# Quarter-row gathers and 32x32 block transposes on VectorE for 44 of 64 experts

## The chip, the core and the metric

The kernel runs on one core of a Trainium2 chip. The core has a matrix engine (TensorE, PE in the profile; its weight loads are listed as PEld), a vector engine (VectorE, DVE), an activation engine (ScalarE, ACT), a general engine (GpSimd, POOL) and a sequencer that here only issues transfers (SyncE, SP). They run side by side, each through its own instructions in order, and wait for one another through semaphores. Sixteen DMA engines move data; SP, ACT and POOL put transfers on queues for them. Data lie in device memory (DRAM), in SBUF (128 partitions), or in PSUM, where TensorE writes its results. The metric is the time of one execution on the device in microseconds (us).

## The reference

One block of a transformer with adaptive normalisation, in float32, for 2048 tokens of 512 features:

```
h = layernorm(x) * (1 + ca) + sa
x = x + ga * attention(h)            # 16 heads of 128, causal
h = layernorm(x) * (1 + cb) + sb
x = x + gb * ffn(h)
```

and `ffn` is a mixture of 64 experts with two shared ones:

```
topk_scores, topk_idx = top_k(softmax(flat @ Wr + router_bias), 4)   # 4 of 64 experts per token
xb[e, pos] = flat[tok]                     # at most 128 tokens per expert
h  = silu(xb @ Wg) * (xb @ Wu)             # 512 -> 128, per expert
yb = h @ Wd                                # 128 -> 512
out[tok] += yb[eid, pos] * weight
hs = silu(flat @ Sg) * (flat @ Su)         # two shared experts of width 512
out += hs @ Sd
```

## The kernel before, in words

The first two thirds of the time are attention: projections, scores, softmax and weighted values, head by head. Its probabilities are transposed by VectorE in 32x32 blocks (`turn_blocks`, L466) after DMAs have swapped the blocks (L456); this is the one place where the kernel before uses that instruction.

**Router stage.** For each tile of 128 tokens, PE sums the attention's output over the heads (L936), VectorE adds it up and normalises it to `h` (`norm`, L747 to L763), and POOL's queue writes `h` to a DRAM tensor `h2d` (L762). `h` has four buffers. `turn_h` transposes `h` on PE into `h2T`, `logit` gives the router's logits, `choose`, `positions` and `seat_tokens` give every token a seat with its experts. After the last tile, `table` is copied to `tb`, and `tok` (L888) holds, for seat p of expert e, the number of the token. SP loads the attention's output for later tiles in this stage (`load_ab`, L572, tile `v`), the shared weights (L932, L933) and then the first three experts' weights.

**Experts.** An expert's rows are gathered by `load_xb` (L1211): an indirect DMA on POOL's queue reads 128 rows of 2 KB of `h2d` at the indices `tok[:, e]`, into one of three buffers `xb`, with a token on each partition. TensorE needs the features on the partitions, so `expert_turn` transposes four 128x128 pieces on PE into the PSUM tile `tpx` (L1221), and ACT copies them to `xbT` (L1223). `expert_up` (L1228) multiplies with the expert's two up weights `wgu` into the PSUM tile `pse`, which has one buffer; `glu` forms `he` from it (L987 on ACT, L988 and L989 on VectorE). `expert_mid` transposes `he` (L1243, `tph`), `expert_down` multiplies with `wd` (L1249, `psy`), VectorE scales it to `y` (L1251), and ACT's queue writes it to DRAM. The steps overlap: step e gathers for e + 3, transposes for e + 1, does the up projection of e, the middle of e - 1 and the down projection of e - 2.

**Order.** The order of these blocks is set in the program, not by priorities. Each step is a list of pairs (columns of PE work, function), and `merge` interleaves the list of the experts with that of the shared experts' work (`first` to `fourth`, tile `pst`, and `shared_down`, tile `psd`) so that both are done by the same share at any time. The cost 512 of a transpose counts in this. `tpx` and `tph`, like `table` before them, have the PSUM tag `tr` with two buffers.

**Combination.** When the experts are done, indirect DMAs gather the results by token (L1281), VectorE adds them up, and SP stores the output, beside the last shared work on PE.

Of the kernel before, what the change touches and what calls it, by code (L numbers as in the profile page):

```python
# [18 lines left out]
P = 128  # L19
# [4 lines left out]
def adaln_block_kernel(  # L24
# [41 lines left out]
    dram = ctx.enter_context(tc.tile_pool(name="dram", bufs=1, space=DRAM))  # L66

    ident = const.tile([P, P], F32)
# [9 lines left out]
    gb = const.tile([P, D], F32)  # L78
    atd = dram.tile([H, DH, N], F32)
    h2d = dram.tile([N, D], F32)  # L80
    ybd = dram.tile([E * CAP, D], F32)

    def merge(streams, marks):
# [40 lines left out]
    with ExitStack() as att:  # L124
# [63 lines left out]
        with tc.tile_pool(name="pre", bufs=1) as pre, tc.manual_schedule():  # L188
# [388 lines left out]
        xts = {}  # L577
# [113 lines left out]
    keep = ctx.enter_context(tc.tile_pool(name="keep", bufs=1))  # L691
# [8 lines left out]
    psO = ctx.enter_context(tc.tile_pool(name="psO", bufs=2, space=PSUM))  # L700
# [5 lines left out]
    rt = rts.enter_context(tc.tile_pool(name="rt", bufs=1))  # L706
# [4 lines left out]
    iota = rt.tile([P, E], F32)  # L711
    places = rt.tile([P, CAP], F32)
    own = rt.tile([P, 1], F32)
    tok = keep.tile([CAP, E], U32)
    hs_ = {}
    mvs = {}
    logits = {}
# [5 lines left out]
    def route_consts():  # L723
        nc.sync.dma_start(out=wr, in_=Wr.rearrange("(k p) e -> p k e", p=P))
        nc.sync.dma_start(out=rb, in_=router_bias.partition_broadcast(P))
        make_upper_triangular(nc, before, val=1.0, diag=False)
        nc.gpsimd.memset(onesb, 1.0)
        nc.gpsimd.iota(
            iota, pattern=[[1, E]], base=0, channel_multiplier=0,
            allow_small_or_imprecise_dtypes=True,  # L730
        )
        nc.gpsimd.iota(
            places, pattern=[[1, CAP]], base=0, channel_multiplier=0,
            allow_small_or_imprecise_dtypes=True,
        )
        nc.gpsimd.iota(
            own, pattern=[[0, 1]], base=0, channel_multiplier=1,
            allow_small_or_imprecise_dtypes=True,
        )

    def load_x(j):
        nc.sync.dma_start(
# [4 lines left out]
    def norm(t):  # L747

        st = rt.tile([P, 6], F32, name="st", bufs=3)
        nc.vector.bn_stats(st, acc[:, t, :])  # L750
        mv = rt.tile([P, 2], F32, name="mv", bufs=3)
        nc.vector.bn_aggr(mv, st)
        rstd = rt.tile([P, 1], F32, name="rstd", bufs=3)
        nc.scalar.activation(rstd, mv[:, 1:2], AF.Sqrt, bias=eps, scale=1.0)
        nc.vector.reciprocal(rstd, rstd)
        h = rt.tile([P, D], F32, name="h", bufs=4)
        nc.vector.tensor_scalar(
            h, acc[:, t, :], mv[:, 0:1], rstd, ALU.subtract, ALU.mult
        )
        nc.vector.tensor_mul(h, h, cb)  # L760
        nc.vector.tensor_add(h, h, sb)
        nc.gpsimd.dma_start(out=h2d[t * P : (t + 1) * P, :], in_=h)  # L762
        hs_[t] = h  # L763

    def turn_h(t):
# [105 lines left out]
    def seat_tokens(b):  # L871


        t0, nt = BLOCKS[b]
        seat, who = seats.pop(b)
        for n in range(nt * K):
            i, k = divmod(n, K)
            nc.tensor.matmul(
                out=table,
                lhsT=seat[:, n, :],  # L880
                rhs=who[:, i, k].rearrange("p j e -> p (j e)"),
                start=(b == 0 and n == 0),
                stop=(b == len(BLOCKS) - 1 and n == nt * K - 1),
            )
        if b == len(BLOCKS) - 1:
            tb = rt.tile([CAP, 2 * E], F32, name="tb")
            nc.vector.tensor_copy(tb, table)
            nc.vector.scalar_tensor_tensor(  # L888
                tok, tb[:, E:], float(P), tb[:, :E], ALU.mult, ALU.add
            )  # L890

    table = psO.tile([CAP, 2 * E], F32, name="table", tag="tr")
    ALL = ((0, 4), (4, 8), (8, 12), (12, 16))
# [12 lines left out]
    with tc.manual_schedule():  # L906
# [55 lines left out]
    with ExitStack() as ex:  # L962
# [241 lines left out]
        xbs = {}  # L1204
        xts = {}
        ups = {}
        hts = {}

        def load_xb(e):
            xbs[e] = xbp.tile([CAP, D], F32, name="xb", bufs=3)  # L1210
            nc.gpsimd.indirect_dma_start(  # L1211
                out=xbs[e][:, :],
                out_offset=None,
                in_=h2d[:, :],
                in_offset=bass.IndirectOffsetOnAxis(ap=tok[:, e : e + 1], axis=0),
            )

        def expert_turn(e):
            tp = psO.tile([P, DC, P], F32, name="tpx", tag="tr")
            for k in range(DC):  # L1220
                nc.tensor.transpose(tp[:, k, :], xbs[e][:, k * P : (k + 1) * P], ident)  # L1221
            xts[e] = xbp.tile([P, DC, CAP], F32, name="xbT")
            nc.scalar.copy(xts[e], tp)  # L1223

        def expert_up(e):
            ps = psO.tile([P, 2 * HE], F32, name="pse", tag="pl", bufs=1)
            for k in range(DC):
                nc.tensor.matmul(  # L1228
                    out=ps,
                    lhsT=xts[e][:, k, :],  # L1230
                    rhs=weights[e][:, k].rearrange("p i h -> p (i h)"),
                    start=(k == 0),
                    stop=(k == DC - 1),
                )
# [19 lines left out]
        def expert_step(e):  # L1254
            out = []

            def turn():
                if e + 3 < E:
                    load_xb(e + 3)
                expert_turn(e + 1)  # L1260

            def down():
                expert_down(e - 2)
                if e + 1 < E:
                    load_down(e + 1)

            if e + 1 < E:
                out.append((512, turn))
            if e < E:
                out.append((1024, lambda: expert_up(e)))  # L1270
            if 0 <= e - 1 < E:
                out.append((128, lambda: expert_mid(e - 1)))
            if e >= 2:
                out.append((512, down))
            return out
# [20 lines left out]
                store(t)  # L1296

        with tc.manual_schedule():
            for e in range(3):
                load_xb(e)  # L1300
            expert_turn(0)
            for j in range(1, 5):
                weight_sum(0, j)
            experts = []
            for e in range(E + 2):
                experts += expert_step(e)
            merge([experts, shared[LEAD:-TAIL]], [])
# [58 lines left out]
```

## Time and profile before

| | |
|---|---|
| median of 9 runs | 2494.81 us (2490.94 to 2496.55) |
| the profiled execution | 2488.51 us, span of its instructions 2486.7 us |
| granted TensorE clock, mean | 0.995 |
| PE busy | 2421.2 us, 97% of the span |
| DVE busy | 1518.7 us, 61% |
| ACT busy | 656.2 us, 26% |
| POOL busy | 224.4 us, 9% |
| gathers of rows, L1211 | 64, 1988.9 to 2329.1 us |
| transposes of gathered rows, L1221 | 256, 1993.4 to 2346.5 us |

An instruction's line in the profile names its engine, its line in the program (L1221), its operation, the tile it writes and those it reads (`tpx<-ident,xb`), and the shape. In lists of groups, the count follows, then the busy time, the mean duration in ns, and after a bar how long the engine stood idle just before these instructions and what ended that. In timelines a line begins with the start and the duration in us, and several instructions of one kind are put together (x4). A float32 matmul has two records, a transpose one. Durations of matmuls overlap, since they are pipelined. A row of the table by windows has the bounds of the window, its length, the busy time of each engine (with the number of instructions), the granted clock, the DMA engines' mean busy share and the GB/s they moved. A row of a DMA queue has packets, MB, and the share of 16 engines' time: q1 carries what SP issues, q0 what POOL issues, q10 what ACT issues. SPq, ACTq and the like are transfers being issued.

### The profile page before, as it was taken

What the parts mean: (1) busy time and instruction counts of PE and PEld (TensorE: products, weight loads), DVE (VectorE), ACT (ScalarE), POOL (GpSimd) and SP (SyncE); (2) the same over time, 40 slices, a digit from 0 to 9 for tenths busy, and PEclk for the clock granted to TensorE, in tenths of its full rate; (3) what the DMA queues carried; (4) which work ended last, traced back from release to release, by engine and by line L of the source; (5) the groups of instructions that cost most, each with busy time, mean ns of one, the idle gap of its engine ahead of it and who ended that gap; (6) DMA issues with size and microseconds to landing.
All of it is one profiled execution on the core that took longest, in us unless ns stands there. A gap on an engine that the chain in (4) does not pass through costs nothing.

```text
span 2486.7 us, 26246 instructions
## 1 busy us (share of the span) xinstructions
PE 2421.2 (97%) x8525; PEld 1524.7 (61%) x8525; DVE 1518.7 (61%) x2982; ACT 656.2 (26%) x1476; POOL 224.4 (9%) x286
## 2 busy tenths in 40 slices
PE   7999999999999999999999999899999999999999
PEld 4666666666666666666666666555544476877844
DVE  4466666676666666666666666676665562654654
ACT  3233333323322333333233333322111221222200
POOL 0000000000000000000000000000100021111073
PEclk9999999999999999999999999999999999999999
DMA  4234434444444444444444344565523277877664
GB/s 140 62 87 108 115 92 111 116 111 103 115 110 97 110 115 98 109 99 119 104 96 121 96 117 110 139 192 139 178 68 131 85 211 219 241 222 237 187 191 147
DMA packets 225952, 326.26 MB, mean 131 GB/s; under 512 B 32116, under 2 KB 140696, under 8 KB 225816
## 3 DMA queue, kind: packets, MB, share of 16 engines
q1 hardware_dynamic: 198936, 253.26, 39.3%
q0 software_dynamic: 17664, 54.54, 7.3%
q10 hardware_dynamic: 9216, 16.78, 1.8%
q8 instruction: 69, 1.13, 0.2%
q14 instruction: 67, 0.55, 0.1%
HBM read 139.91 MB, written 41.94 MB: 73 GB/s over the span
## 4 chain that ended last, share of the span: by engine, by line
PE 70%; DVE 16%; SPq 6%; issue 3%; DMA 3%; ACT 1%; POOL 1%; DVEq 0%; ACTq 0%; POOLq 0%
PE pqk L169 12%; PE ps L413 12%; PE po L484 11%; PE pso L936 6%; DVE pt L466 6%; PE pv L329 6%; SPq L456 6%; PE pse L1228 4%; PE pst L1083 4%; DVE nm L426 3%; PE psd L1145 3%; PE psg L999 3%; DVE p L402 2%; PE psy L1249 2%; PE psb L591 2%
## 5 line engine op out<-in xcount | busy, mean ns | idle before, releaser
L432 ACT ACTIVATE p<-ps,nm 128x1024 f32<-128x1024 f32 (+7 forms) x384 | 332.0, 864 | 1039.8 <-DVE nm L430 370.7
L484 PE MATMUL po<-pt,v 128*128 128x256 f32 (+1 forms) x2304 | 567.4, 368 | 7.3 <-DVE pt L466 3.6
L413 PE MATMUL ps<-kt,qt 128*128 128x512 f32 (+3 forms) x1280 | 532.7, 532 | 32.2 <-ACT p L432 31.3
L484 PEld LDWEIGHTS po<-pt,v 128*128 128x128 f32 x2304 | 425.6, 190 | 222.1 <-issue 156.0
L426 DVE TENSOR_REDUCE nm<-ps 128x1 f32<-128x1024 f32 (+7 forms) x384 | 349.5, 910 | 94.8 <-PE ps L413 86.0
L466 DVE STREAM_TRANSPOSE pt<-pt 128x1664 f32<-128x1664 f32 (+2 forms) x160 | 317.9, 1988 | 59.3 <-DMA pt<-p 54.2
L413 PEld LDWEIGHTS ps<-kt,qt 128*128 128x128 f32 x1280 | 234.8, 190 | 181.8 <-issue 127.3
L425 DVE TENSOR_TENSOR ps<-ps,causal 128x128 f32<-128x128 f32 x256 | 74.4, 291 | 348.8 <-PE ps L413 348.7
L329 PE MATMUL pv<-wv,hT 128*128 128x256 f32 x1024 | 240.3, 379 | 0.0
L169 PE MATMUL pqk<-hT,wk 128*128 128x512 f32 x512 | 233.2, 599 | 0.0
L169 PE MATMUL pqk<-hT,wq 128*128 128x512 f32 x512 | 231.7, 596 | 0.0
L494 POOL DMA_DIRECT2D atd<-at x128 | 79.1, 619 | 1676.5 <-ACT at L493 1653.6
L402 DVE TENSOR_SCALAR p<-p,rs 128x1024 f32<-128x1024 f32 (+7 forms) x384 | 218.0, 596 | 9.1
L329 PEld LDWEIGHTS pv<-wv,hT 128*128 128x128 f32 x1024 | 194.5, 190 | 31.0 <-issue 1.9
L936 PE MATMUL pso<-hT,v 128*128 128x512 f32 x384 | 173.7, 597 | 0.0
L169 PEld LDWEIGHTS pqk<-hT,wk 128*128 128x128 f32 x512 | 98.5, 193 | 103.6 <-issue 101.0
L169 PEld LDWEIGHTS pqk<-hT,wq 128*128 128x128 f32 x512 | 97.8, 191 | 98.4 <-issue 95.4
L1228 PE MATMUL pse<-wgu,xbT 128*128 128x256 f32 x512 | 121.1, 379 | 0.0
L936 PEld LDWEIGHTS pso<-hT,v 128*128 128x128 f32 x384 | 69.6, 190 | 71.5 <-issue 70.8
L1145 PE MATMUL psd<-wsd,hs 128*128 128x512 f32 x256 | 111.5, 592 | 0.0
L1228 PEld LDWEIGHTS pse<-wgu,xbT 128*128 128x128 f32 x512 | 93.8, 190 | 11.7 <-issue 1.0
L1211 POOL DMA_INDIRECT xb<-h2d,tok x64 | 65.0, 1015 | 302.1 <-PE tpx L1221 273.1
(258 smaller groups left out, 1930.2 us busy)
## 6 DMA issues: line engine op xcount, KB each, us to landing
pt<-p SPq DMA_DIRECT2D x768, 104.0 KB
pt<-p SPq DMA_DIRECT2D x256, 124.0 KB
pt<-p SPq DMA_DIRECT2D x256, 108.0 KB
atd<-at POOLq DMA_DIRECT2D x128, 128.0 KB
wgu<-in_L_ffn_Wg_dram SPq DMA_DIRECT2D x64, 256.0 KB
wgu<-in_L_ffn_Wu_dram SPq DMA_DIRECT2D x64, 256.0 KB
wd<-in_L_ffn_Wd_dram SPq DMA_DIRECT2D x64, 256.0 KB
ybd<-y ACTq DMA_DIRECT2D x64, 256.0 KB
```

Of the source, the lines that this page charges most:

```text
L169: nc.tensor.matmul(out=ps, lhsT=w[:, k, :], rhs=hTs[j][:, k, :], start=(k == 0), stop=(k == DC - 1),)
L329: nc.tensor.matmul(out=ps, lhsT=hTs[t // 4][:, k, (t % 4) * P : (t % 4 + 1) * P], rhs=wv[:, k].rearrange("p i d -> p (i d)"), start=(k == ...
L402: nc.vector.tensor_scalar(cols[:, :, a:b], cols[:, :, a:b], rs[:, n : n + 1], None, ALU.mult)
L413: nc.tensor.matmul(out=ps[:, o : o + wo], lhsT=q, rhs=kts[hd, (c0 + o) // 512][:, :wo], start=True, stop=True,)
L426: nc.vector.tensor_reduce(nm[:, n : n + 1], ps[:, :w], AX.X, ALU.max, negate=True)
L432: nc.scalar.activation(rows[:, r0 + c0 // P : r0 + (c0 + w) // P], ps[:, :w].rearrange("q (r b k) -> q r b k", b=4, k=32), AF.Exp, bias=nm ...
L456: nc.sync.dma_start(out=pt[32 * b : 32 * (b + 1), a * w : (a + 1) * w], in_=pb[32 * a : 32 * (a + 1), b * w : (b + 1) * w],)
L466: nc.vector.transpose(part, part)
L484: nc.tensor.matmul(out=po if wide else po[:, P:], lhsT=vts[g][:, kt, hh * DH : (hh + 1) * DH], rhs=rows[:, r : r + last + 1 : last] if wid ...
L936: nc.tensor.matmul(out=ps, lhsT=abs_[pr][:, hd, i * P : (i + 1) * P], rhs=wos[hd // 4][:, hd % 4, :], start=(hd == 0), stop=(hd == H - 1),)
L1145: nc.tensor.matmul(out=ps, lhsT=hsh[b, f][:, i * P : (i + 1) * P], rhs=wsd[:, f, :], start=(f == 0), stop=(f == NHC - 1),)
L1228: nc.tensor.matmul(out=ps, lhsT=xts[e][:, k, :], rhs=weights[e][:, k].rearrange("p i h -> p (i h)"), start=(k == 0), stop=(k == DC - 1),)
```

## The change

Experts 0 to 5 and every fourth from 8 on (`whole`) are handled as before; that is 20 of 64. For the other 44:

- `norm` writes every tile of `h` a second time, to `h2q`, with four DMAs on SP's queue. There a token's row of 512 features is stored in four quarter rows of 128: quarter b holds, for each of the four blocks of 128 features, the 32 features b x 32 to b x 32 + 31.
- `load_xb` issues four indirect DMAs of 128 quarter rows (512 B each), one per group of 32 seats. Partition 32 q + s gets, in column block b, quarter q of the token in seat 32 b + s. The indices are `tokq`: four times the token's number, plus the quarter.
- `expert_turn` transposes the gathered tile with one VectorE instruction in 32x32 blocks, straight from SBUF to `xbT` in SBUF, with no PE and no ACT work. Its cost in `merge` is 0 instead of 512.
- To make `tokq`, the seat numbers of `tb` have to be repeated on other partitions: four small matmuls with selection matrices `pick` (copied by POOL from the identity) and one VectorE instruction, after `tok`.

For all experts `xb` gets a fourth buffer, and a step gathers for e + 4 instead of e + 3.

```diff
+    h2q = dram.tile([N, D], F32)
...
+    quarter = rt.tile([P, 1], F32)
+    pick = rt.tile([P, 4, 4, 32], F32)
     tok = keep.tile([CAP, E], U32)
+    tokq = keep.tile([P, 4, E], U32)
...
+        for b in range(4):
+            nc.gpsimd.memset(quarter[32 * b : 32 * (b + 1), :], float(b))
+            nc.gpsimd.tensor_copy(pick[:, :, b, :], ident.rearrange("p (t r) -> p t r", r=32))
...
         nc.gpsimd.dma_start(out=h2d[t * P : (t + 1) * P, :], in_=h)
+        for b in range(4):
+            nc.sync.dma_start(
+                out=h2q[t * P : (t + 1) * P, b * P : (b + 1) * P].rearrange(
+                    "p (k d) -> p k d", d=32
+                ),
+                in_=h.rearrange("p (k b d) -> p b k d", b=4, d=32)[:, b],
+            )
...
             nc.vector.scalar_tensor_tensor(
-                tok, tb[:, E:], float(P), tb[:, :E], ALU.mult, ALU.add
+                tb[:, :E], tb[:, E:], float(P), tb[:, :E], ALU.mult, ALU.add
             )
+            nc.vector.tensor_copy(tok, tb[:, :E])
+            ps = psO.tile([P, 4, E], F32, name="psq", tag="tr")
+            for b in range(4):
+                nc.tensor.matmul(
+                    out=ps[:, b, :],
+                    lhsT=pick[:, b].rearrange("p a r -> p (a r)"),
+                    rhs=tb[:, :E],
+                    start=True,
+                    stop=True,
+                )
+            nc.vector.tensor_scalar(tokq, ps, 4.0, quarter, ALU.mult, ALU.add)
...
+        def whole(e):
+            return e < 6 or e % 4 == 0
+
         def load_xb(e):
-            xbs[e] = xbp.tile([CAP, D], F32, name="xb", bufs=3)
...
+            else:
+                xbs[e] = xbp.tile([P, D], F32, name="xb", bufs=4)
+                for b in range(4):
+                    nc.gpsimd.indirect_dma_start(
+                        out=xbs[e][:, b * P : (b + 1) * P],
+                        out_offset=None,
+                        in_=h2q.rearrange("n (b f) -> (n b) f", b=4),
+                        in_offset=bass.IndirectOffsetOnAxis(ap=tokq[:, b, e : e + 1], axis=0),
+                    )
 
         def expert_turn(e):
...
+            else:
+                xt = xbp.tile([P, DC, CAP], F32, name="xbT")
+                nc.vector.transpose(
+                    xt.rearrange("p k (b s) -> p b k s", s=32),
+                    xbs[e].rearrange("p (b k s) -> p b k s", b=4, s=32),
+                )
+                xts[e] = [xt[:, k, :] for k in range(DC)]
...
-                if e + 3 < E:
-                    load_xb(e + 3)
+                if e + 4 < E:
+                    load_xb(e + 4)
                 expert_turn(e + 1)
...
-                out.append((512, turn))
+                out.append((512 if whole(e + 1) else 0, turn))
...
-            for e in range(3):
+            for e in range(4):
                 load_xb(e)
```

More of the change, by code (lines that the diff above doesn't have):

```diff
@@ L1207, in adaln_block_kernel @@
         hts = {}
+        def whole(e):
+            return e < 6 or e % 4 == 0
         def load_xb(e):
-            xbs[e] = xbp.tile([CAP, D], F32, name="xb", bufs=3)
[L1211 to L1216, printed above, removed]
-        def expert_turn(e):
[L1219 to L1223, printed above, removed]
+            if whole(e):
+                xbs[e] = xbp.tile([CAP, D], F32, name="xb", bufs=4)
+                nc.gpsimd.indirect_dma_start(
+                    out=xbs[e][:, :],
+                    out_offset=None,
+                    in_=h2d[:, :],
+                    in_offset=bass.IndirectOffsetOnAxis(ap=tok[:, e : e + 1], axis=0),
+                )
+            else:
+                xbs[e] = xbp.tile([P, D], F32, name="xb", bufs=4)
+                for b in range(4):
+                    nc.gpsimd.indirect_dma_start(
+                        out=xbs[e][:, b * P : (b + 1) * P],
+                        out_offset=None,
+                        in_=h2q.rearrange("n (b f) -> (n b) f", b=4),
+                        in_offset=bass.IndirectOffsetOnAxis(ap=tokq[:, b, e : e + 1], axis=0),
+                    )
+        def expert_turn(e):
+            if whole(e):
+                tp = psO.tile([P, DC, P], F32, name="tpx", tag="tr")
+                for k in range(DC):
+                    nc.tensor.transpose(tp[:, k, :], xbs[e][:, k * P : (k + 1) * P], ident)
+                xt = xbp.tile([P, DC, CAP], F32, name="xbT")
+                nc.scalar.copy(xt, tp)
+                xts[e] = [xt[:, k, :] for k in range(DC)]
+            else:
+                xt = xbp.tile([P, DC, CAP], F32, name="xbT")
+                nc.vector.transpose(
+                    xt.rearrange("p k (b s) -> p b k s", s=32),
+                    xbs[e].rearrange("p (b k s) -> p b k s", b=4, s=32),
+                )
+                xts[e] = [xt[:, k, :] for k in range(DC)]
         def expert_up(e):
@@ L1229, in expert_up @@
                     out=ps,
-                    lhsT=xts[e][:, k, :],
+                    lhsT=xts[e][k],
                     rhs=weights[e][:, k].rearrange("p i h -> p (i h)"),
```

## The prediction

> **What bounds the kernel now.** I read the page's busy times first, then the stage with the experts in the table of busy times by window, then its groups of instructions, its timeline, and the DMA queues of that stage.
>
> ```profile
> span 2486.7 us, 26246 instructions
> PE 2421.2 (97%) x8525; PEld 1524.7 (61%) x8525; DVE 1518.7 (61%) x2982; ACT 656.2 (26%) x1476; POOL 224.4 (9%) x286
> ```
>
> The experts run from 1994 us (first transpose of gathered rows) to 2352 us (last up projection). By window:
>
> ```profile
> core 0: us, PE busy (x) PEld busy (x) DVE busy (x) ACT busy (x) POOL busy (x), PEclk, DMA share, GB/s
> 2050.00:2110.00 60.00, 60.00 (x227) 37.56 (x226) 15.87 (x36) 11.27 (x32) 10.39 (x11) 1.00 0.71 214
> 2110.00:2170.00 60.00, 60.00 (x285) 48.35 (x284) 36.96 (x91) 14.89 (x40) 11.59 (x11) 1.00 0.84 246
> sum 360.00, PE 360.00 PEld 266.84 DVE 183.84 ACT 83.07 POOL 63.88; mean PE 60.00 PEld 44.47 DVE 30.64 ACT 13.84 POOL 10.65
> ```
>
> PE has no gap in 360 us (the sum runs over six windows from 1990 to 2350); DVE is busy half of it, POOL a sixth, and the DMA engines 71 to 84%. So PE is the bound of this stage, and DMA has the smallest margin. The timeline of one tightly packed step, with nothing of the shared experts between, shows what a transpose costs PE and how long the chain beside it is:
>
> ```profile
> 2070.29 1.02 PE L1249 MATMUL psy<-wd,heT 128*128 128x512 f32 x2
> 2071.15 0.60 PE L1221 MATMUL tpx<-ident,xb 128*128 128x128 f32 x4
> 2071.58 1.89 PE L1228 MATMUL pse<-wgu,xbT 128*128 128x256 f32 x8
> ...
> 2073.51 0.28 ACT L987 ACTIVATE sig<-pse 128x128 f32<-128x128 f32 x1 [0.43 <-PE pse L1228]
> 2073.82 0.29 DVE L988 TENSOR_TENSOR sig<-sig,pse 128x128 f32<-128x128 f32 x1 [1.78 <-ACT sig L987]
> 2074.14 0.29 DVE L989 TENSOR_TENSOR he<-sig,pse 128x128 f32<-128x128 f32 x1
> 2074.28 0.60 PE L1221 MATMUL tpx<-ident,xb 128*128 128x128 f32 x4
> ...
> 2074.72 0.60 PE L1228 MATMUL pse<-wgu,xbT 128*128 128x256 f32 x2
> ```
>
> Durations of matmuls overlap; starts tell the pitch. From the transposes' start to that of the next matmul is 0.43 us (2071.15 to 2071.58): this is what four transposes hold PE. The 38.2 us busy of the group, 0.60 us per expert, counts overlap twice. The second thing to see: pse has one PSUM buffer, and DVE reads it until 2074.43; the next pse starts at 2074.72.
>
> **The change part by part.**
>
> (a) Removed from PE. 20 experts stay whole (0 to 5 and 8, 12, ... 60), 44 are changed. 44 x 0.43 = 18.9 us, on the path. Ends: 0 (all of it turned into waits) and 44 x 0.60 = 26.3 us (busy time). I take 18.9, since starts tell the pitch.
>
> (b) Where the stall comes back. In the built order of instructions nine pairs of consecutive pse are left with only tph and psy between. From the pse start at 2071.58, the next was 3.14 us later; without tpx it would be 2.71 us, but DVE's last read of pse ends at 2.85 us and the weight load comes some 0.15 us after it. So such a step keeps about 3.0 us, losing 0.3 of its 0.43: 9 x 0.3 = 2.7 us. Ends 0 and 9 x 0.43 = 3.9.
>
> (c) Added to DVE: 44 transposes of 128x512. The attention's rows give the price.
>
> ```profile
> L466 DVE STREAM_TRANSPOSE pt<-pt x160: 1899/1912/2247, 106.3 to 1747.4; 128x1664 f32<-128x1664 f32 x96, 128x1984 f32<-128x1984 f32 x32, 128x1728 f32<-128x1728 f32 x32
> ```
>
> 1912 ns for 1664 columns and 2247 for 1984 is 1.05 ns a column, so 512 columns cost 1.912 - 1152 x 0.00105 = 0.70 us (an estimate: here the block order is strided, which no row shows; the upper end is the whole 1.9 us). 44 x 0.70 = 31 us raise DVE from 184 to 215 us of a stage of some 345 us. The transpose of expert e+1 stands in DVE's queue ahead of sig and he of expert e, and y and the sums of the shared units stand behind it. In a packed step DVE idles 1.78 us ahead of sig, which covers 0.70. In steps with a shared unit the second part of a unit issues six DVE operations of 0.42 us (2.5 us) just ahead, and 16 steps now have 2.68 us of PE work between two pse; there the cover is thin. I allow 3.0 us: about a third of these 16 steps, 0.6 us each. Ends: 0, and 31 us if every transpose were exposed; nearer to 0, as DVE still has 130 us idle.
>
> The Trainium skill's "VectorE: DVE Perf Modes", Rules for kernel authors, sends a 128x128 transpose to TensorE when PSUM will do as its destination. Engine time here agrees, 0.43 against 0.70 us. By that rule alone the change would lose 44 x 0.27 = 12 us; the windows above say that the two engines' time is not worth the same.
>
> (d) Removed from ACT: 44 copies of 0.585 us. ACT is at 83 of 360 us, so worth nothing by itself; it clears ACT's queue ahead of sig.
>
> (e) POOL: 44 gathers become 176.
>
> ```profile
> L1211 POOL DMA_INDIRECT xb<-h2d,tok x64: 942/944/1442, 1988.9 to 2329.1; - x64
> ```
>
> The first two gathers start 1.37 us apart (1988.87, 1990.24), so four take 5.5 us at worst. Three changed experts and a whole one are 18 us of POOL, against 4 x 5.3 = 21 us of PE. Hidden, at 85%. What waits behind them is the next gather only; DVE's transposes wait for the landing. The tile pool has four buffers instead of three and the load runs four experts ahead, and eight software DMAs share eight semaphores, each waiting for the one eight before; eight issues take 10 us, longer than a landing. Price 0; lower end 0, upper end see the rivals.
>
> POOL issues keep 944 ns median with DVE busy half of the time, and stretch to 1442 at most. The Trainium skill's "SBUF — State Buffer", SBUF: two separate sides, speaks against the change: a DVE instruction that takes both ports locks GpSimd out, and a software DMA of 620 ns took 3100. By that, an estimate, four gathers would take 12.4 us, 44 of them 546 us, and POOL would bound the stage some 200 us later than now.
>
> (f) DMA. 256 KB per gather stay, in rows of 512 B instead of 2 KB.
>
> ```profile
> q1 hardware_dynamic: 72902, 47.64, 46.6%
> q0 software_dynamic: 4720, 15.47, 17.5%
> q10 hardware_dynamic: 8640, 15.73, 12.0%
> ```
>
> These are the queues from 2000 to 2350 us: 59 gathers took 17.5% of 350 us, 1.04 us each. On q1 a packet, mostly 512 B of wgu, takes 0.466 x 16 x 350 / 72902 = 36 ns; 512 such rows take 512 x 0.036 / 16 = 1.15 us. So 0.1 us more per gather, 5 us over the stage, which has 24% of 350 = 84 us free: hidden. Ends: 0, and four times 1.04 if a row costs the same at any size (+3.1 us each, 137 us). I take 0.1, from the row that moves 512 B.
>
> (g) h2q: 64 more DMAs on SP in the router stage, four per token tile, 512 pieces of 128 B each: 32768 packets. At no more than the 36 ns above they add 74 us of 16 engines between 1766 and 1965 us, where DMA is 27% busy after 1782. SP now waits for each h before it issues the next loads; a tile's four issues at about 0.6 us (the row of pt loads) and the normalisation of some 5 us put the loads of v some 8 to 10 us later. They have two tiles' time, about 31 us, and need about 6: hidden. Expert weights start behind h2q of the last tile, some 8 us later than 1955, and are needed at 1996: hidden. h has four buffers; the fifth waits for the first h2q behind two 1 MB loads, up to 3 us of DVE at 1780, which idles 4.7 us at 1788. Price 0; ends 0 and 10 us.
>
> (h) psq: four matmuls of 128x64 and the wait for tb. PE would go on at 1986.95 after table; tb is ready at 1987.85, so 1.0 us of wait and 0.9 us for four (logits of the same shape take 1.00 us busy for eight records): 1.9 us on the path. tok comes 0.2 us later, ahead of a gather that PE does not yet wait for.
>
> (i) The built order changes at the last tile: DVE's hs, which waited 1.75 us for PE, moves behind the normalisation of h.
>
> ```profile
> 1959.38 0.69 DVE L989 TENSOR_TENSOR hs<-sig,psg 128x512 f32<-128x512 f32 x1 [1.75 <-PE psg L999]
> 1962.32 1.08 PE L768 MATMUL tp<-ident,h 128*128 128x128 f32 x4 [2.98 <-DVE h L761]
> ```
>
> h can start when rstd is there at 1958.15 instead of 1959.98, so PE's gap of 2.98 us shrinks by 1.5 us (0 to 1.8).
>
> **Sum**: -18.9 + 2.7 + 3.0 + 1.9 - 1.5 = -12.8 us. The profiled execution took 2488.51 us (span 2486.7), 6.3 below the median 2494.81; against itself it would become 2475.7. Off the median: 2482.0 us.
>
> **The rivals.** A measurement of this kernel can tell about 0.2% (5 us) from no change.
> - DMA becomes the bound, slower. If gathering small rows costs by the row, PE waits for weights in the packed stretches. DMA work is 0.76 x 350 = 266 us, the PE stage becomes about 337 us; it decides once a quarter gather costs more than 1.04 + 71/44 = 2.7 us. At three times today's cost (+92 us) the stage takes 358 us, 8 more than now: about 2503. At four times, 403 us: about 2548. For it: 0.84 in one window. Against: 36 ns per 512 B packet.
> - DVE becomes late. With half of its 31 us exposed, -18.9 + 2.7 + 15.5 + 0.4 leaves nothing: about 2494.5, no change. With all of it, or at 1.9 us a transpose, about 2510. For it: DVE's queue is in order and he gates the next pse. Against: 130 us idle.
> - POOL binds: at 1.37 us each no; from 1.9 us each (4 x 1.9 x 3 + 1.9 = 25 us against 21) yes, some 2 us per group of four behind today (16 groups): about 2530.
> - The change does only part: transposes go but the shared work is spread otherwise, so that more steps are packed; -5 us, about 2490.
>
> **How the numbers follow.** Forecast case 0.62 (2474 to 2489); DMA or POOL bound 0.12 (2495 to 2550); DVE late 0.18, of which half near no change and half slower; partial gain 0.08, half of it under 5 us. Faster: 0.62 + 0.02 = 0.64; no change: 0.15; slower: 0.21. The range 2472 to 2508 leaves out about 0.1 above and 0.05 below (gain by busy time).
>
> **What would show it.** Right: 80 transposes tpx on PE, PE still without gaps, the expert stage about 13 us shorter, 44 DVE transposes of 0.7 us. Wrong: PE waiting for wgu or for xbT (DMA, POOL), a long wait of pse on he (DVE), sums of waits over 5 us in the router stage (h2q), or DVE's transposes far above 0.7 us.

## The result: slower, and the profile after

| | before | after |
|---|---|---|
| median, lowest to highest | 2494.59 us (2489.35 to 2500.84, 34 runs) | 2506.58 us (2500.49 to 2514.06, 11 runs) |
| the profiled execution (span) | 2488.51 us (2486.7) | 2510.64 us (2508.9) |
| start of the first pse to start of the last psy, the expert stage | 362.2 us | 381.9 us |
| from there to the end | 128.0 us | 130.6 us |

The ratio is 1.0052, with a 95% interval of 1.0043 to 1.0060: 0.5% slower, where 0.5% faster was forecast. The two profiled executions lie further apart than the medians, 22.2 us of span against 12.0, so the profiles show more than the usual loss. The page of the kernel before has one line on pse:

```profile
L1228 PE MATMUL pse<-wgu,xbT 128*128 128x256 f32 x512 | 121.1, 379 | 0.0
```

The page of the changed kernel has:

```profile
span 2508.9 us, 26211 instructions
PE 2414.0 (96%) x8357; PEld 1509.2 (60%) x8357; DVE 1544.2 (62%) x3028; ACT 630.6 (25%) x1431; POOL 347.7 (14%) x426
L1255 POOL DMA_INDIRECT xb<-h2q,tokq x176 | 169.6, 964 | 152.0 <-DVE xbT L1272 70.9
L1281 PE MATMUL pse<-wgu,xbT 128*128 128x256 f32 x512 | 126.0, 390 | 15.2 <-issue 6.3
```

PE lost work as forecast, but it now stands idle ahead of pse for 15.2 us, where before it never did (0.0). The instructions that read or write xbT give the price of VectorE's transposes:

```profile
L1272 DVE STREAM_TRANSPOSE xbT<-xb x44: 695/701/705, 2023.9 to 2365.5; 128x512 f32<-128x512 f32 x44
```

The busy times by window say where the time went. Here are four of the six windows used before, and the sum of all six:

```profile
core 0: us, PE busy (x) PEld busy (x) DVE busy (x) ACT busy (x) POOL busy (x), PEclk, DMA share, GB/s
2050.00:2110.00 60.00, 58.01 (x201) 34.97 (x200) 21.80 (x45) 7.29 (x27) 30.69 (x33) 1.00 0.73 225
2110.00:2170.00 60.00, 52.63 (x224) 40.94 (x223) 36.82 (x90) 9.45 (x28) 30.12 (x32) 0.97 0.70 213
2170.00:2230.00 60.00, 50.89 (x215) 38.95 (x214) 37.89 (x89) 8.85 (x27) 29.06 (x32) 0.97 0.66 197
2290.00:2350.00 60.00, 54.36 (x227) 42.41 (x225) 31.79 (x76) 8.72 (x27) 32.52 (x34) 0.94 0.71 214
sum 360.00, PE 335.35 PEld 237.58 DVE 191.40 ACT 54.30 POOL 187.91; mean PE 55.89 PEld 39.60 DVE 31.90 ACT 9.05 POOL 31.32
```

PE had 60.00 of 60 in each before. Now 24.65 of 360 us are gaps, and the granted clock falls below 1.00 in three windows: it is at half from 2133.9, 2209.0 and 2304.6 us on, each time some microseconds after a gap of PE of 3 us or more began (2125.3, 2205.0, 2302.5 us). No engine has become the bound: DVE is busy 53%, POOL 52%, the DMA engines less than before (0.70 against 0.84 from 2110 to 2170). The timeline around one gap shows what the engines waited for. Each line has start, duration, engine, line, operation and tiles; in brackets the idle time before it.

```profile
2119.43 1.03 PE L1111 MATMUL pst<-ts,ws 128*128 128x256 f32 x4
2120.29 0.27 PE L1296 MATMUL tph<-ident,he 128*128 128x128 f32 x1
2120.40 1.02 PE L1302 MATMUL psy<-wd,heT 128*128 128x512 f32 x2
...
2123.42 1.89 PE L1281 MATMUL pse<-wgu,xbT 128*128 128x256 f32 x8
2123.77 0.94 POOL L1255 DMA_INDIRECT xb<-h2q,tokq  x1 [0.30 <-issue]
2125.02 0.95 POOL L1255 DMA_INDIRECT xb<-h2q,tokq  x1 [0.31 <-issue]
2128.37 0.37 ACT L1121 COPY p<-pst 128x256 f32<-128x256 f32 x1 [5.28 <-remote]
2128.44 0.34 SPq L1010 DMA_DIRECT2D wd<-in_L_ffn_Wd_dram  x1
2128.64 0.27 ACT L1298 COPY heT<-tph 128x128 f32<-128x128 f32 x1
2128.74 0.95 POOL L1246 DMA_INDIRECT xb<-h2d,tok  x1 [2.77 <-remote]
...
2128.96 0.33 PE L1296 MATMUL tph<-ident,he 128*128 128x128 f32 x1 [3.65 <-ACT heT L1298]
```

By its rows PE finished pst at 2120.46 and psy at 2121.42. ACT's copy of pst begins 7.9 us after the one, SP's next load of wd, which waits for the other, 7.0 us after it. Everything that waits for PE starts within 0.4 us, at 2128.4, and PE itself, waiting for ACT, loses 3.65 us. Meanwhile PE's matmuls went on starting at their usual pitch, until the last of pse at about 2125. In the trace's record of PE's semaphore no signal is noted between 2121.98 and 2128.35 us, and then six within 0.32 us. This record alone proves little, since it has holes: from 2113.45 to 2118.43 us it notes nothing either, yet ACT's heT began 0.1 us after its tph (2115.37 after 2115.28). The late starts of ACT, SP and POOL do show that the word of PE's finish came late. Whether the results themselves reached PSUM late behind those starts, the records cannot tell. The Trainium skill's "Perfetto Trace Analysis", Per-engine timelines, says that the end in a TensorE record is an estimate and that the semaphore update follows once PSUM has acknowledged the write, outside of what is reported. This trace agrees that such a stretch exists, up to 7.9 us here, and cannot be read from PE's rows; it has to be read from the starts of those who wait.

As a measure I take, for each of the 64 experts, the time from the end of the last pse matmul to the start of ACT's sig, which waits for it ("the lag" below). Before: median 0.04 us, longest 1.02 us. After: longest 6.69 us, 10 of 64 over 2 us. The lag also holds what ACT has ahead of sig in its queue: in the longest one ACT had begun again at 2128.37 us, and sig started at 2132.01. The word of ACT's sig to VectorE was never late: the step from the end of ACT's sig, or from when VectorE was free, to VectorE's sig (L1016 after the change) took at most 0.03 us for all 64 experts, before and after. The 12 gathers POOL had issued in an unbroken row, 1.25 us apart, from 2111.2 us on ended some 0.7 us after PE's gap began; before, one pair of gathers started 1.25 us apart, at 1994.7 us, and from 2000 us on all were at least 3.1 us apart.

### The profile page after: what moved, and what is told of

It reads as the page before. It is cut to its first block, busy times and chain, and to the rows that moved or that the text cites. A ratio compares the mean times of both kernels' runs of the same rounds, so it can differ in the third digit from the quotient of the medians.

```text
span 2508.9 us, 26211 instructions
## 1 busy us (share of the span) xinstructions
PE 2414.0 (96%) x8357; PEld 1509.2 (60%) x8357; DVE 1544.2 (62%) x3028; ACT 630.6 (25%) x1431; POOL 347.7 (14%) x426
## 4 chain that ended last, share of the span: by engine, by line
PE 67%; DVE 16%; SPq 6%; issue 3%; DMA 3%; another core or an unknown queue 2%; ACT 2%; POOL 0%; DVEq 0%; ACTq 0%; POOLq 0%
PE ps L416 12%; PE pqk L172 12%; PE po L487 11%; DVE pt L469 6%; PE pso L964 6%; PE pv L332 5%; SPq L459 5%; PE pse L1281 4%; PE pst L1111 4%; DVE nm L429 3%; PE psd L1173 3%; DVE p L405 2%; PE psg L1027 2%; PE psb L594 2%; PE psy L1302 2%
## 5 line engine op out<-in xcount | busy, mean ns | idle before, releaser
L416 PEld LDWEIGHTS ps<-kt,qt 128*128 128x128 f32 x1280 | 235.2, 190 | 182.3 <-issue 128.0
L1255 POOL DMA_INDIRECT xb<-h2q,tokq x176 | 169.6, 964 | 152.0 <-DVE xbT L1272 70.9
L1281 PE MATMUL pse<-wgu,xbT 128*128 128x256 f32 x512 | 126.0, 390 | 15.2 <-issue 6.3
## 6 DMA issues: line engine op xcount, KB each, us to landing
atd<-at POOLq DMA_DIRECT2D x128, 128.0 KB
```

Of the source, the lines that this page charges most:

```text
L416: nc.tensor.matmul(out=ps[:, o : o + wo], lhsT=q, rhs=kts[hd, (c0 + o) // 512][:, :wo], start=True, stop=True,)
L1255: nc.gpsimd.indirect_dma_start(out=xbs[e][:, b * P : (b + 1) * P], out_offset=None, in_=h2q.rearrange("n (b f) -> (n b) f", b=4), in_offse ...
L1281: nc.tensor.matmul(out=ps, lhsT=xts[e][k], rhs=weights[e][:, k].rearrange("p i h -> p (i h)"), start=(k == 0), stop=(k == DC - 1),)
```

## The experiments

Everything below is compared with runs of the kernel before on the same chip, in the same set. One thing was found on the way and is needed to read the rest: the kernel before took 2482 to 2483 us in some sets and 2494 us in the others, medians of one sort within about 0.05% of each other. I call the first **place A** and the second **place B**; the result above is of place B. The number of the chip does not decide it: chip 1 was place B in the third set and A in the fourth and the last.

### First set: which part of the change (place A, before 2481.9 us)

The first theories were G (the gathers), D (VectorE's queue), O (the merge price 0) and R (the router's part). One gather instead of four:

```
-                for b in range(4):
-                    nc.gpsimd.indirect_dma_start(out=xbs[e][:, b * P : (b + 1) * P], ...
-                        in_offset=...IndirectOffsetOnAxis(ap=tokq[:, b, e : e + 1], axis=0))
+                nc.gpsimd.indirect_dma_start(out=xbs[e][:, :], out_offset=None, in_=h2q[:, :],
+                    in_offset=bass.IndirectOffsetOnAxis(ap=tok[:, e : e + 1], axis=0))
```

> The changed kernel with one gather of 128 whole rows (2 KB) in place of the four quarter gathers of a changed expert; VectorE still transposes, TensorE still does not, the order is untouched. Left out: the right placing of the rows, so the changed experts work on wrongly ordered numbers of the same size. Theory G (the four gathers hold the core up: their bursts of 9 to 12 on POOL, 15 us long, end where PE stands still): the stalls go, the expert stage keeps the gain of TensorE, 2478 to 2486 us. Theory D (VectorE's transposes stand ahead of sig and he in its queue): nothing changes, 2503 to 2510 us. Theory O (the merge price of 0 for the changed steps lets psd and expert steps fall badly): nothing changes, 2503 to 2510 us. Theory R (the writes of the quarter table and the router's added work): nothing changes.

Measured: 2462.6 us, ratio 0.9925 (0.9911 to 0.9939).

```
         def expert_turn(e):
-            if whole(e):
+            if True:
...
-                out.append((512 if whole(e + 1) else 0, turn))
+                out.append((512, turn))
```

> The changed kernel with its quarter gathers, but every expert transposed by TensorE and copied out by ScalarE as before, at the merge price of 512. Left out: the blocks are not put back in order, so the changed experts work on wrongly ordered numbers. Theory G: all of the gathers' loss and none of TensorE's gain, some 18 us or more above the kernel before, 2510 to 2525 us. Theory D: as before, 2493 to 2498 us. Theory O: as before, 2493 to 2498 us. Theory R: some 2505 us.

Measured: 2481.3 us, ratio 0.9994 (0.9985 to 1.0003).

```
         def whole(e):
-            return e < 6 or e % 4 == 0
+            return True
```

> The changed kernel with all 64 experts loaded by one whole gather and transposed by TensorE: only the quarter table h2q, the quarter lists, the fourth xb buffer and the load four experts ahead are left of the change. Theories G, D and O: within 3 us of the kernel before, 2491 to 2497 us (the router's part priced at +0.4 us in the prediction). Theory R: 2500 us or more.

Measured: 2481.9 us, ratio 0.9997 (0.9988 to 1.0006). Its expert stage is 362.2 us long, as before.

```
-                out.append((512 if whole(e + 1) else 0, turn))
+                out.append((512, turn))
```

> The changed kernel whole, but the step of a changed expert is priced at 512 columns in the merge as before, so that shared work and experts interleave as they did. Theory G: still held up by the gathers, 2498 to 2510 us. Theory D: 2500 to 2510 us. Theory O: the gain of TensorE comes out, 2476 to 2485 us. Theory R: 2503 to 2510 us.

Measured: 2465.7 us, ratio 0.9932 (0.9918 to 0.9945).

This looked like theory O: the price restored, the gain is there. But it did not fit together: one_gather kept price 0 and gained as well, four_pe kept the gathers and lost nothing. And the kernel before had taken 12.7 us more in the result than here. So the unaltered change had to run beside the two.

### Second set: the same once more (place B, before 2494.0 us)

No edit: the changed kernel, and cost512 and one_gather as above.

> The changed kernel once more, unaltered, beside the two that follow. Theory O (the loss comes of the merge price 0 together with the four gathers): slower than before by 10 to 14 us again, with 20 us or more of idle TensorE in the expert stage. Theory M (the stalls hang on the place where it ran, not on the order: the median of before was 2494.6 us there and 2481.9 us in the four runs of the first set): on a chip where before takes 2482 us the changed kernel takes 2463 to 2468 us, with under 2 us of idle TensorE in the expert stage; on one where before takes 2494 us it is slower again, and so is the one at price 512.

Measured: 2506.4 us, ratio 1.0047 (1.0032 to 1.0061); 25.4 us of gaps in PE in the expert stage.

> The changed kernel at the merge price of 512, once more. Theory O: 14 to 18 us faster than before wherever it runs. Theory M: level with the changed kernel of this set to 4 us, whichever way that one goes.

Measured: 2505.4 us, ratio 1.0051 (1.0036 to 1.0067). The same program was 0.7% faster than before at place A and is 0.5% slower here. Theory O is refuted; the price moves the time by nothing that can be measured (1.0 us beside the changed kernel of this set).

> One gather of whole rows in place of four, once more (rows wrongly placed, as said). Theories O and M both: 17 to 21 us faster than before; should it stall too, neither holds.

Measured: 2472.8 us, ratio 0.9907 (0.9890 to 0.9923), with 1.0 us of gaps in the stage. With one gather the gain is there at both places, though VectorE transposes all the same. Theories D and R are refuted with it, as this kernel has both.

### Third set: what of the gathers (place B, before 2494.3 us)

> The changed kernel unaltered, as the control of this set. What is known so far: where before takes 2494 us this kernel takes 2506 us and the same kernel at price 512 2505 us; where before takes 2482 us the one at price 512 takes 2466 us, and this one was not run there. Theory M (the chip decides, not the order): 2504 to 2509 us beside a before of 2494 us, 2462 to 2468 us beside a before of 2482 us.

Measured: 2504.4 us, ratio 1.0052 (1.0035 to 1.0069).

> Quarter gathers with TensorE's transposes and the old price (blocks not put back in order, so the changed experts work on wrongly ordered numbers). Beside a before of 2482 us: 2480 to 2483 us as in the first set. Beside a before of 2494 us it tells two theories apart. The gathers alone hold TensorE up: 2515 to 2525 us, with 20 us and more of idle TensorE in the expert stage. Only the gathers together with VectorE's transposes do: 2492 to 2497 us.

Measured: 2503.9 us, ratio 1.0041 (1.0027 to 1.0054): 9.6 us lost, under the 21 us and more that "gathers alone" expected, and over the 3 us at most of the other theory. PE has 7.1 us of gaps in the six windows, where "gathers alone" expected 20 and more. Its profiled execution, 2495.5 us, was the quickest of the six. The window in which it lost most, first here and then at place A (columns as above):

```profile
2230.00:2290.00 60.00, 53.25 (x204) 33.73 (x202) 15.26 (x34) 9.60 (x27) 32.05 (x34) 1.00 0.68 210
```

```profile
2230.00:2290.00 60.00, 60.00 (x238) 39.33 (x237) 20.90 (x48) 11.51 (x34) 34.65 (x37) 1.00 0.81 246
```

The same program, without VectorE's transposes and in the old order, has PE at 60.00 in one place and 53.25 in the other. So the gathers alone suffice at place B. They cost more in the changed kernel: beside one gather (2472.8 us), four cost 33.6 us there (2506.4 us, same set) and 10 us here. In the profiled execution this kernel has 3 rows of nine or more gathers (starts at most 1.6 us apart), the changed kernel of the result 9; that this is why was only argued, and the same program has 9 such rows at place A, where it loses nothing.

```
         def whole(e):
-            return e < 6 or e % 4 == 0
+            return e < 6 or e % 2 == 0
```

> The changed kernel with every other expert from the eighth on changed, not three of four: 29 changed experts, 5 gathers for two experts instead of 13 for four. TensorE's part is 29 of 44 of the gain. Beside a before of 2494 us: if the loss goes with the number of quarter gathers, 8 us slower than before, 2500 to 2504 us; if it comes only when POOL issues almost without a pause, 8 to 11 us faster than before, 2483 to 2486 us. Beside a before of 2482 us: 2470 to 2474 us.

Measured: 2493.6 us, ratio 0.9995 (0.9981 to 1.0009), between the two expectations. Two stalls are left, of 2.9 us each, at 2114.5 and 2284.0 us, each some microseconds after a row of nine gathers (from 2098.9 and 2268.3 us). Two more rows of nine (from 2053.6 and 2236.2 us) left no lag over 1.6 us, so a row does not stall PE each time.

```
                 for b in range(4):
                     nc.gpsimd.indirect_dma_start(
-                        out=xbs[e][:, b * P : (b + 1) * P], ...
+                        out=xbs[e][32 * b : 32 * b + 32, :], out_offset=None, in_=h2q[:, :],
+                        in_offset=bass.IndirectOffsetOnAxis(ap=tok[:32, e : e + 1], axis=0),
```

> The changed kernel with four gathers for a changed expert that bring 32 whole rows of 2 KB each, in place of 128 quarter rows of 512 B each: as many gathers and bytes, a quarter of the rows to be looked up. All four take the first 32 rows of the list, so the changed experts work on the wrong rows. Beside a before of 2494 us: if the number of gathers holds TensorE up, 2500 to 2510 us; if the number of looked-up rows does (176 gathers of 128), 2470 to 2476 us as with one gather. Beside a before of 2482 us: 2460 to 2468 us.

Measured: 2516.9 us, ratio 1.0094 (1.0078 to 1.0109). The gathers' line of this run:

```profile
L1255 POOL DMA_INDIRECT xb<-h2q,tok x176: 856/865/1361, 2000.8 to 2355.8; - x176
```

A gather of 32 rows holds POOL 0.865 us, one of 128 rows 0.947 us. A quarter of the looked-up rows in as many gathers cost no less, so it is not the rows that count. Back to back these gathers start 1.17 us apart, closer than the 1.25 us of the changed kernel; that this makes them worse is argued.

### Fourth set: the control at place A (before 2482.5 us)

> The changed kernel unaltered, the control of this set. Beside a before of 2494 us: 2504 to 2507 us. Beside a before of 2482 us: 2462 to 2468 us if the chip decides; over 2490 us if the merge price matters after all.

Measured: 2463.3 us, ratio 0.9927 (0.9915 to 0.9940). **The changed kernel, unaltered, is 0.7% faster than before at place A and 0.5% slower at place B.** Two of its windows at place A and the sum of the six, beside those of the result above:

```profile
2110.00:2170.00 60.00, 60.00 (x270) 48.27 (x269) 44.41 (x105) 12.24 (x36) 35.31 (x37) 1.00 0.84 257
2170.00:2230.00 60.00, 59.91 (x235) 41.99 (x234) 36.21 (x83) 8.89 (x29) 34.76 (x36) 1.00 0.73 222
sum 360.00, PE 358.99 PEld 260.64 DVE 222.20 ACT 61.38 POOL 192.51; mean PE 59.83 PEld 43.44 DVE 37.03 ACT 10.23 POOL 32.08
```

And the same spot of the timeline:

```profile
2116.35 1.03 PE L1111 MATMUL pst<-ts,ws 128*128 128x256 f32 x4
2117.21 0.27 PE L1296 MATMUL tph<-ident,he 128*128 128x128 f32 x1
...
2117.28 0.94 POOL L1255 DMA_INDIRECT xb<-h2q,tokq  x1 [0.30 <-issue]
2117.32 1.02 PE L1302 MATMUL psy<-wd,heT 128*128 128x512 f32 x2
2117.41 0.37 ACT L1121 COPY p<-pst 128x256 f32<-128x256 f32 x1 [0.64 <-PE pst L1111]
2117.68 0.27 ACT L1298 COPY heT<-tph 128x128 f32<-128x128 f32 x1
...
2118.38 0.34 SPq L1010 DMA_DIRECT2D wd<-in_L_ffn_Wd_dram  x1
```

The copy of pst follows the matmul by 0.03 us (7.9 at place B), SP's load follows psy by 0.04 us (7.0), with POOL issuing its gathers 1.25 us apart all the while. The longest lag is 0.85 us.

```
                 xbs[e] = xbp.tile([P, D], F32, name="xb", bufs=4)
+                for _ in range(5):
+                    nc.gpsimd.memset(xbs[e], 0.0)
```

> One gather of whole rows per changed expert (rows wrongly placed) and, ahead of it, five memsets of the same buffer on POOL, some 2.6 us by the 0.2 us of a 128x128 memset in the trace of before, in place of the other three gathers' 2.9 us. Beside a before of 2494 us: if a busy POOL delays the others, as slow as the changed kernel, 2500 to 2510 us; if the gathers themselves do, 2470 to 2478 us as with one gather alone. Beside a before of 2482 us: 2460 to 2466 us either way.

Measured: 2463.2 us, ratio 0.9928 (0.9916 to 0.9941).

```
                 for b in range(4):
+                    for _ in range(3):
+                        nc.gpsimd.memset(xbs[e][:, b * P : (b + 1) * P], 0.0)
                     nc.gpsimd.indirect_dma_start(
```

> Every other expert changed (29), and three memsets of 128x128 on POOL ahead of each quarter gather, some 0.6 us, so that quarter gathers start 1.9 us apart in place of 1.25 us. Beside a before of 2494 us: if it takes gathers one right behind the other, the two stalls of the unpaced one go, 2483 to 2488 us; if their number alone counts, 2491 to 2497 us as unpaced. Beside a before of 2482 us: 2470 to 2474 us.

Measured: 2471.8 us, ratio 0.9962 (0.9949 to 0.9975).

```
         def whole(e):
-            return e < 6 or e % 4 == 0
+            return e < 6 or e % 4 != 1
```

> The changed kernel with one expert of four changed (14 experts), 7 gathers for four experts. TensorE's part of the gain is 14 x 0.43 = 6 us. Beside a before of 2494 us: 2487 to 2491 us if so few gathers cost nothing, 2493 to 2498 us if each costs its part. Beside a before of 2482 us: 2475 to 2478 us.

Measured: 2476.6 us, ratio 0.9980 (0.9972 to 0.9989). At place A the gain goes with the number of changed experts: 5.9 us for 14, 19.2 us for 44, some 0.43 us each. What it does at place B was not tried.

### Fifth set: POOL's time or the gathers, and their distance (place B, before 2494.3 us)

> One gather and five memsets on POOL per changed expert (rows wrongly placed), once more, for a chip where before takes 2494 us. If a busy POOL delays the others, 2500 to 2510 us; if the gathers themselves do, 2470 to 2478 us as with one gather alone. Should the chip be one where before takes 2482 us: 2463 us as in the last set, and the question stays open.

Measured: 2469.0 us, ratio 0.9899 (0.9884 to 0.9913). The instructions on xb, and the sum over the six windows:

```profile
L1255 POOL MEMSET xb<- x220: 524/524/540, 1999.5 to 2311.1; 128x512 f32 x110
...
L1256 POOL DMA_INDIRECT xb<-h2q,tok x44: 951/951/1292, 2002.6 to 2311.9; - x44
```

```profile
sum 360.00, PE 359.00 PEld 260.68 DVE 221.97 ACT 61.34 POOL 180.24; mean PE 59.83 PEld 43.45 DVE 37.00 ACT 10.22 POOL 30.04
```

POOL is busy 180 us here and 188 us in the changed kernel, and PE has 1.0 us of gaps against 24.65. A POOL busy with memsets delays nobody; the gathers do.

> Every other expert changed, quarter gathers held apart by memsets, once more, for a chip where before takes 2494 us. If it takes gathers one right behind the other, 2483 to 2488 us; if their number alone counts, 2491 to 2497 us as unpaced. Should the chip be one where before takes 2482 us: 2472 us as in the last set.

Measured: 2484.6 us, ratio 0.9970 (0.9960 to 0.9980), against 0.9995 without the memsets. The window of the first stall, unpaced and then paced:

```profile
2110.00:2170.00 60.00, 57.08 (x252) 45.51 (x252) 40.01 (x97) 12.00 (x35) 22.54 (x24) 0.97 0.75 225
```

```profile
2110.00:2170.00 60.00, 60.00 (x275) 48.33 (x274) 42.13 (x103) 13.36 (x37) 40.66 (x94) 1.00 0.82 242
```

With as many gathers, but 2.19 us apart (median) in place of 1.25, the stalls in the expert stage are gone: longest lag 1.78 us, against 3.61. So it takes gathers close behind one another. (Paced and unpaced at place B stand in two sets, on chips 13 and 1, each beside its own runs of before.) This version is faster than before at both places, by 10.7 and 9.7 us.

### Last run: all 44, held apart a little (place A, before 2483.1 us)

```
                 for b in range(4):
+                    nc.gpsimd.memset(xbs[e][:, b * P : (b + 1) * P], 0.0)
                     nc.gpsimd.indirect_dma_start(
```

> The changed kernel whole, 44 changed experts, with one memset of 128x128 on POOL ahead of each quarter gather: gathers some 1.6 us apart, by the 2.19 us that three memsets gave and the 1.25 us of none. Thirteen for four experts then take some 20.5 us of their 22.4 us. Beside a before of 2494 us: 2468 to 2478 us if this distance is enough, 2495 to 2507 us if it takes more. Beside a before of 2482 us: 2462 to 2467 us, and the question stays open.

Measured: 2462.3 us, ratio 0.9918 (0.9905 to 0.9932), gathers 1.44 us apart. This is level with the changed kernel's at place A by the intervals, so the memsets cost nothing there. Whether 1.44 us is enough at place B stays open.

### What the kernel before loses at place B

Of its 12 us between the places the two profiled executions show 7.0, none in the expert stage (362.2 us in both; router_only stands for before at place A, where before has no trace). They lie behind it, where the 64 gathers of the combination stand in rows. The window from 2390 to 2420 us, first before at place B, then router_only, which equals it in time, at place A:

```profile
2390.00:2420.00 30.00, 25.29 (x51) 10.60 (x50) 17.72 (x26) 1.19 (x2) 20.97 (x20) 0.89 0.66 195
```

```profile
2390.00:2420.00 30.00, 30.00 (x71) 13.30 (x70) 22.27 (x32) 1.79 (x3) 23.60 (x22) 1.00 0.75 223
```

After the last psy the one needs 128.0 us and the other 121.0. That this has the same cause as the stalls above fits, but no run separates it, and the other 5 us are in no profile.

## Why the prediction was wrong, point by point

**(a) TensorE, 44 x 0.43 us: right.** 80 tpx are left, and where nothing else interferes (place A) the expert stage shrinks from 362.2 to 345.6 us.

**(b) Packed steps keep about 3.0 us: right.** They were 3.14 us from pse to pse; the nine that lost a tpx take 2.94 to 3.06 us at place A. (a) and (b) together said -16.2 us, the stage shows -16.6.

**(c) VectorE: price right, allowance not needed.** 0.701 us each, as estimated. Of the 3.0 us for lateness at most the 1.0 us of gaps at place A came. The rival "DVE late" is out. The rule quoted from the Trainium skill's "VectorE: DVE Perf Modes" would have cost 12 us; at place A the whole change gains 19, since TensorE's time was the bound (60.00 of 60 us busy before) and VectorE had time to spare.

**(e) POOL, price 0: the step that failed.** It said that what waits behind the gathers is the next gather only, and looked for a bound in POOL's own time. At place A that holds: four_pe is level with before. At place B four gathers per expert cost 9.6 us with TensorE's transposes and 33.6 us beside one gather with VectorE's, at POOL prices no higher than forecast (0.95 us, 1.25 us from start to start against 1.37, 52% busy). The cost fell on the word of PE's finish to ACT, VectorE, SP and POOL, and on PE through them. In the profiled execution at place B, the stage is 381.9 - 345.6 = 36.3 us longer than at place A: 25.4 us of it are more gaps in PE (26.4 against 1.0), 6.8 us come from 13.7 us at half clock after such gaps, and 4.1 us are left without an account. One window of the trace of before might have warned: that from 2390 to 2420 us, where gathers stand in rows and PE has 4.7 us of gaps. The prediction did not use it, since the change does not touch that stage. The lock of the Trainium skill's "SBUF — State Buffer", SBUF: two separate sides, weighed there, did not show: the gathers kept 947 ns median beside VectorE's transposes.

**(f) DMA: hidden, as said.** From 2000 to 2370 us queue q0 took this of the 16 engines:

```profile
q0 software_dynamic: 6752, 15.22, 14.6%
```

That is 0.93 us for 256 KB (54.0 us for 15.22 MB) against 1.04 before, where 0.1 more was forecast; the small rows cost nothing, and the DMA rival is out.

**(g), (h), (i): right in sum.** +0.4 us was said, router_only is 0.0 us off with (g) and (h) in it. At place A the expert stage of the changed kernel begins 1.1 us sooner than router_only's.

**The sum.** For place A, -12.8 us was forecast and -19.2 measured. By the profiles, with router_only for before, 3.0 of the difference is (c), 0.4 the stage beyond (a) and (b), 2.0 the start of the stage and the time after it (-1.6 against +0.4), and 1.0 lies between the profiled executions and the medians. For place B, that of the result, +12.0 was measured against -19.2 at place A: the sum lacked a term of some 31 us, which (e) had put at 0. (In the chances, half of 0.08 is 0.04 and not the 0.02 that was added to 0.62.) The rival "POOL binds" had the right engine and the wrong mechanism: PE never waited for a gather's landing worth mentioning, and POOL was idle half of the time. No rival had one engine's gathers delay the word of another engine's finish.

**What is not settled.** What makes a place A or B, and what holds up the word of PE's finish. The profiles tell the places apart (the signals missing from the record, last section) but not why.

## What to carry to other kernels

Indirect gathers issued one right behind the other can cost engines that have nothing to do with them; look at how many stand in a row (a row of seven in the run with 32 rows each, from 2000.8 to 2008.0 us, was enough for a lag of 5.08 us; two of four rows of nine with every other expert changed left none over 1.6 us), not only at POOL's busy time, and hold them apart with short POOL instructions if there is room (2.19 us apart left no stall here). Where an engine stands idle for "remote" or "issue" in several places at once, compare the end of the work waited for with the start of those who wait. And repeat the unaltered change beside every set of experiments: a verdict of half a per cent had one sign in one place and the other sign in the next.

## What the runs showed of the hardware that was not expected

- The lag from the end of pse to ACT's sig (ACT's own queue included), over 64 experts each, longest and number over 2 us:

| | place A | place B |
|---|---|---|
| before (router_only at A) | 1.02 us, 0 | 1.02 us, 0 |
| four gathers, changed kernel | 0.85 us, 0 | 6.69 us, 10 |
| four gathers, changed kernel at price 512 (cost512) | 0.96 us, 0 | 5.79 us, 15 |
| four gathers, TensorE transposes (four_pe) | 1.02 us, 0 | 6.41 us, 7 |
| four gathers of 32 rows | | 9.64 us, 11 |
| one gather, VectorE transposes | 0.85 us, 0 | 0.85 us, 0 |
| one gather and memsets | 0.85 us, 0 | 0.85 us, 0 |

- The price moves no time, but it moves the lags: with price 512 more experts are late at place B (15 against 10), though none as late as in the changed kernel.
- The record of signals differs between the places. Up to 1985 us every trace has one for each instruction of PE, ACT and VectorE that gives one. From the first gathers on, all nine traces of place A have at least as many, and all eleven of place B lack some: before 18 of ACT's 239 and 24 of VectorE's 475, the changed kernel 71 of PE's 327, 63 of ACT's 195 and 168 of VectorE's 514. One gather per expert lacks fewer (19, 8 and 55). What their absence means the traces do not tell, since ACT's word of sig to VectorE was not late.
- At place B the three profiled executions of the changed kernel have their two longest gaps in the expert stage at the same experts: 3.65, 3.62 and 3.56 us at 2125 to 2127 us, 3.55, 3.58 and 3.53 us at 2204 to 2205 us. It is no random disturbance.
- A gather by index holds POOL 0.947 us for 128 rows of 512 B, as long as for 128 rows of 2 KB (0.944 in the trace of before), and 0.865 us for 32 rows of 2 KB; back to back they start 1.25 us apart.
